# List products in the masks' slots, and a regrouped routing tail, in a masked-attention and expert kernel

## The chip, the cores and the metric

The kernel runs on one core of a Trainium2 chip. A core has five engines that run side by side, each through its own list of instructions in order: TensorE (PE, with PEld for its weight loads) multiplies matrices, VectorE (DVE) works elementwise, ScalarE (ACT) copies and applies functions, GpSimd (POOL) fills constants and issues the indirect DMAs, and SyncE (SP) issues DMAs. [...] ACT issues DMAs too, in its own order. The metric is the device time of one execution in microseconds (us); a comparison is made of several executions of each kernel.

## The reference, cut to what matters

The input `x` is 4096 rows of 512; `adj` is a 4096 x 4096 matrix of zeros and ones with few ones, denser in its first rows.

```python
adj = max(adj, eye)
q, k, v = layernorm(x) @ Wqs, Wks, Wvs          # 8 heads of 64
scores = q k^T / 8 + 0.01 * eye - 1e16 * (1 - adj)
x = x + sum_h softmax(scores) v Wo              # attention
xf = layernorm(x)
logits = xf @ Wg + bg                           # 8 experts
topk_scores, topk_idx = top_k(logits, 2)
w = softmax(topk_scores)
h = gelu(xf W1[e] + b1[e]);  y = h W2[e] + b2[e]
x = x + w[0] * y[topk_idx[0]] + w[1] * y[topk_idx[1]]
```

Only scores where `adj` is one count, and of the eight experts only two per row. The kernel computes just these.

## The kernel before, in words

Rows are handled in 32 tiles of 128. The work has three stages.

**Stage one** normalises `x`, projects it to keys, values and queries and writes them to DRAM (`kv_d`, `q_d`), and at the same time reads `adj` and makes of it, for every tile of queries, a list of the keys that it needs. It is paced by the f32 projections on PE. A slot is one program-level product of 128x512 (two passes in the trace); there are 384. Before each product `step()` runs the jobs that are registered for its slot (`job(slot, f)`), in the order in which they were registered, so the source writes every engine's order by hand. For chunk `h` of `adj` (four tiles of rows by 512 columns, 64 chunks) slot 5 + 5h holds `masks` (L478: four 16-bit products with 32-column weights), three slots later `turn_masks`. After eight chunks a group `g` of four tiles is complete; its jobs hang on slot `s` = 5 + 5h + 5: classes, counts, ranks (`places`, at s to s+8), then the lists (`group_lists`): `rows` and `values` on DVE, 16 one-hot tiles on DVE (`hot`, L281, five buffers), 16 sets of 16-bit products with 32-column weights on PE (`quads`, L294), a copy on ACT (`copy`, L303), and a transpose and key steps (`keys`, L308 to L315). A group follows another every 40 slots.

```python
job(s + 9, call, hold, "l", 0)              # rows
job(s + 10, call, hold, "l", 1)             # values
for x2 in range(NT // 2):
    job(s + 11 + 2 * x2, call, hold, "l", 2, x2)       # hot
    job(s + 16 + x2 // 2 * 4, call, hold, "l", 3, x2)  # quads
job(s + 44, call, hold, "l", 4)             # copy
job(s + 47, call, hold, "l", 5)             # keys
```

**Attention** takes two list steps at a time (a duo). GpSimd gathers the listed keys and values into a ring of 24 places in SBUF (L696); the ring lies where stage one's buffers were. PE turns the keys (L723), multiplies queries by keys (L760), ACT applies the exponential (L767), DVE the mask (L773), PE multiplies by values (L788). The main loop puts `scores` of the next duo, `turn` of the one three ahead and `values` of the present one, then the jobs registered with `at(n, i, job)` for this step. PSUM has three banks for all of this, taken in turn (`bank`).

When a tile of queries is done, `end_of` scales it (L810 to L812), turns it, projects it with `wo` (L828), adds `x` (L837), writes the row out and takes the statistics. When a group of tiles is done (seven of four tiles, then tiles 28 and 29, 30, and 31), `route` makes the second layernorm (`root`, `norm`, in place in the tile of `x`), the logits (`flip`, `gate`), the rank of each expert in a row (`rank`), its place in the expert's list (`place`, `number_places`, `keep_places`), the first and second choice (`pick(0)`, `pick(1)`: six DVE steps each; `weigh`: the difference of the two logits on DVE and its exponential on ACT, L1010 and L1011), the weights (`finish`), and the scatter of every row to the lists of its two experts in DRAM (`scatter`, L1029, on GpSimd, two per tile). A row carries four further words: its number, the place of its first choice, and the two weights. After the last group `totals` counts the rows for each expert and pads each list's end with a tile of blank rows: three on GpSimd, three on SP, two on ACT (L970, L985). The loop's steps past the last duo have no attention work.

Then the table of expert tiles is made on DVE with one product on PE (L1146 to L1182), a flag is computed (L1186 to L1198), and the **expert stage** begins: SP fetches the first four tiles (`fetch`, L1226), PE runs 60 transposes that serve nothing else (`warm`, L1296), DVE goes on with the table for half tiles (`halves`), and then for each of 66 tiles PE turns the rows (L1301), multiplies (L1341), turns (L1352), multiplies (L1370), and GpSimd adds the result into the output (L1392).

## Time and profile before

| what | us |
|---|---|
| median of three runs (2056.35 to 2059.91) | 2056.84 |
| the profiled execution | 2068.36 |
| its span in the trace | 2066.5 |
| PE busy | 1942.0 (94%) |
| DVE busy | 959.3 (46%) |
| ACT busy | 785.1 (38%) |
| GpSimd busy | 571.1 (28%) |
| stage one's last f32 product | about 465 |
| last step of attention's value products | about 1487 |
| first product of the expert stage | 1531.4 |

How to read it. The page's second part cuts the span into 40 slices; a digit is an engine's busy share in tenths, and the row of the clock gives the share of PE's full speed that was granted. In a timeline a row has the start, the length, engine, line, operation, output and inputs, shapes, the number of equal instructions merged, and in brackets the idle time of the engine before it with what ended it. PE's instructions are pipelined and their ends modelled, so one reads the difference of two starts. An engine that is mostly idle can still set the time where others wait for it.

### The profile page before, as it was taken

Reading aid. Unit: us, or ns where it says so; the run is one execution under the profiler, and the core shown is the slowest. Engines: PE = TensorE matmul, PEld = TensorE weight load, DVE = VectorE, ACT = ScalarE, POOL = GpSimd, SP = SyncE. Lnnn points to the kernel's source line nnn. Section 1 sums busy time; section 2 is a strip of 40 time slices with the busy share of each in tenths; the row PEclk is TensorE's granted clock in tenths of the full one; section 3 lists DMA queues with packets and bytes.
Section 4 is the critical chain, followed back from the end, with each engine's and each line's share of the span. In section 5 each row is a group of like instructions: output and inputs, shape, how many; then the busy total and the mean of one; then the engine's idle time right before and its main releaser. Section 6 shows DMA issues by size and latency. Waiting matters only on the chain. (4 is left out here: it accounts for less than half of the span.)

```text
span 2066.5 us, 59701 instructions
## 1 busy us (share of the span) xinstructions
PE 1942.0 (94%) x25491; PEld 1283.8 (62%) x25491; DVE 959.3 (46%) x2501; ACT 785.1 (38%) x1152; POOL 571.1 (28%) x721
## 2 busy tenths in 40 slices
PE   9899999998999998999999998998869999999996
PEld 4344444447888787887878787787644444444443
DVE  3455555534544464564545555464653333333332
ACT  3233233315555554644545454445312222222221
POOL 2000000015333426354272625333121222222221
PEclk9999999999999999999999999999979999999998
DMA  9877877339678849779596777868873555555532
GB/s 371 267 254 255 255 254 243 99 132 406 215 259 286 287 165 366 274 267 318 202 340 234 282 280 259 293 214 305 273 269 77 132 127 111 116 114 118 113 68 42
DMA packets 193410, 462.00 MB, mean 224 GB/s; under 512 B 30384, under 2 KB 46768, under 8 KB 193008
## 3 DMA queue, kind: packets, MB, share of 16 engines
q0 software_dynamic: 67024, 249.44, 37.6%
q1 hardware_dynamic: 101808, 177.51, 26.1%
q10 hardware_dynamic: 24304, 31.11, 4.3%
q8 instruction: 206, 3.38, 0.6%
q14 instruction: 68, 0.56, 0.1%
HBM read 385.37 MB, written 72.64 MB: 222 GB/s over the span
## 5 line engine op out<-in xcount | busy, mean ns | idle before, releaser
L696 POOL DMA_INDIRECT ring<-kv_d,idx x361 | 360.9, 1000 | 873.7 <-ACT l L303 437.1
L767 ACT ACTIVATE pr<-ps 128x1024 f32<-128x1024 f32 x270 | 270.4, 1025 | 376.1 <-PE ps L760 373.9
L773 DVE SCALAR_TENSOR_TENSOR pr<-t,pr 128x1024 f32<-128x1024 uint16 x238 | 284.5, 1223 | 243.8 <-ACT pr L767 243.7
L760 PE MATMUL ps<-q,kT 64*64 64x64 f32 (+1 forms) x10224 | 308.5, 237 | 26.4 <-issue 24.4
L788 PE MATMUL o<-ring,pr 128*64 128x65 f32 x8640 | 297.3, 226 | 26.9 <-issue 24.0
L760 PEld LDWEIGHTS ps<-q,kT 64*64 64x64 f32 (+1 forms) x10224 | 274.8, 149 | 69.5 <-issue 56.4
L788 PEld LDWEIGHTS o<-ring,pr 128*64 128x64 f32 x8640 | 273.9, 140 | 54.6 <-issue 49.4
L1341 PE MATMUL ph<-ring,xT 128*128 (+1 forms) x528 | 238.1, 594 | 0.8 <-ACT xT L1303 0.8
L723 PE MATMUL pkT<-ident,ring 128*128 128x128 f32 x1572 | 206.0, 280 | 12.7 <-DMA ring<-kv_d 6.0
L725 ACT COPY kT<-pkT 128x512 f32<-128x512 f32 (+1 forms) x270 | 198.5, 787 | 15.0 <-DMA q_d<-qT 6.7
L1392 POOL DMA_INDIRECT out_dram<-y,r x66 | 101.8, 1543 | 367.8 <-ACT y L1387 293.3
L723 PEld LDWEIGHTS pkT<-ident,ring 128*128 128x128 f32 x1572 | 171.0, 142 | 29.8 <-issue 7.7
L1370 PE MATMUL py_e<-ring,hT 128*128 (+1 forms) x396 | 182.3, 596 | 1.6 <-ACT hT L1363 1.6
L1341 PEld LDWEIGHTS ph<-ring,xT 128*128 128x128 f32 (+1 forms) x528 | 91.3, 183 | 99.9 <-issue 98.7
L1387 ACT ACTIVATE y<-y,wt 128x512 f32<-128x512 f32 x66 | 47.6, 722 | 269.5 <-DVE y L1383 229.7
L604 PE MATMUL pv<-wv,xT 128*128 128x512 f32 x256 | 131.3, 608 | 0.0
L604 PE MATMUL pk<-wk,xT 128*128 128x512 f32 x256 | 128.8, 614 | 0.7 <-ACT xT L399 0.7
L589 PE MATMUL pq<-xT,wq 128*128 128x512 f32 x256 | 125.9, 607 | 0.0
L1346 DVE COPY h<-ph 128x512 f32<-128x512 f32 x66 | 45.6, 692 | 169.9 <-PE ph L1341 169.9
L1029 POOL DMA_INDIRECT xs_d<-x,slot_i x64 | 70.2, 1097 | 186.6 <-DVE x L1025 159.3
L828 PE MATMUL py<-wo,oT 128*128 128x512 f32 x256 | 118.9, 607 | 1.4 <-ACT oT L822 0.7
L1370 PEld LDWEIGHTS py_e<-ring,hT 128*128 128x128 f32 (+1 forms) x396 | 67.2, 183 | 75.9 <-issue 74.1
(293 smaller groups left out, 1893.3 us busy)
## 6 DMA issues: line engine op xcount, KB each, us to landing
adj<-in_adj_dram SPq DMA_DIRECT2D x64, 1024.0 KB, 5.6
wo<-in_L_ffn_W_dram SPq DMA_DIRECT2D x72, 256.0 KB, 4.6
kv_d<-kvr ACTq DMA_DIRECT2D x32, 516.0 KB, 5.7
ring<-kv_d SPq DMA_DIRECT2D x32, 516.0 KB, 6.9
r<-xs_d SPq DMA_DIRECT2D x57, 258.0 KB, 2.6
ring<-in_L_ffn_W_dram SPq DMA_DIRECT2D x56, 256.0 KB, 5.2
xt<-in_x_dram SPq DMA_DIRECT2D x32, 256.0 KB, 6.3
q_d<-qT ACTq DMA_DIRECT2D x32, 256.0 KB, 2.8
```

The source lines that it names most:

```text
L589: nc.tensor.matmul(pq, w["q"][:, c, ts(p, P)], xTs[b][:, c, :], start=(c == 0), stop=(c == DC - 1),)
L604: nc.tensor.matmul(pk, xTs[b][:, c, ts(t, P)], w[n][:, c, :], start=(c == 0), stop=(c == DC - 1),)
L696: nc.gpsimd.indirect_dma_start(out=g, out_offset=None, in_=kv_d, in_offset=bass.IndirectOffsetOnAxis(ap=idx[i // GL][:, i % GL, a : a + 1] ...
L723: nc.tensor.transpose(pk[:, x * NP + p, :], g[:, ts(p, P)], ident)
L725: nc.scalar.copy(kT[:, : nk * NP], pk[:, : nk * NP])
L760: nc.tensor.matmul(ps[c : c + nk, r, p * P + x * nq : p * P + (x + 1) * nq], kT[r * KD : (r + 1) * KD, p, c : c + nk], q[r * KD : (r + 1) ...
L767: nc.scalar.activation(pr.rearrange("p h q -> p (h q)"), ps.rearrange("p r f -> p (r f)"), AF.Exp)
L773: nc.vector.scalar_tensor_tensor(pr, st["t"].unsqueeze(1).to_broadcast([P, H, P]), 0.0, pr, op0=ALU.is_gt, op1=ALU.mult,)
L788: nc.tensor.matmul(o[c * HALF : (c + 1) * HALF, h // NP, (h % NP) * VW : (h % NP + 1) * VW], pr[:, hd * NP + p, c * HALF : (c + 1) * HALF] ...
L828: nc.tensor.matmul(hold["py"], hold["oT"][:, c, :], wo[:, c, :], start=(c == 0), stop=(c == NP - 1),)
L1341: nc.tensor.matmul(ph[a], xTs[b][:, c, a], w, start=(c == 0), stop=(c == DC - 1), skip_group_check=b >= FULL,)
L1370: nc.tensor.matmul(py[a], hTs[b][:, c, a], w, start=(c == 0), stop=(c == HC - 1), skip_group_check=b >= FULL,)
```

## The change

It has these parts.

- Stage one: `rows` and `values` come one slot later; the products of two one-hot tiles stand at s+15, s+20, ..., s+50, five slots apart, which are the slots of `masks` (they are registered first, so they come directly ahead of them); the one-hots stand at 0 and 2 in each five slots; copy and keys come at s+52 and s+55.
- Routing: `pick` handles both choices in one set of steps of twice the width, with the exponential asked for after the fourth. A row now carries the place of its first choice, 1/(1+e) and e, where e is that exponential; the expert stage makes the weight from these with three steps instead of two. For the last two groups, of one tile each, these words are written straight into the row. The last three tiles' norms go to tiles of their own instead of in place.
- The order behind attention: the choices of tile 30 come one step later, so behind the rank of tile 31; jobs of the last duo's step run before its value products; 24, 8 and 30 transposes of the identity (`idle`) are put on PE after the last projection, after the last rank and after the totals.
- The blank rows: five on SP, and three on ACT behind the last choices; none on GpSimd.
- The table: two constants are made at the kernel's start, and a subtraction and a product become one step.

```diff
@@ -147,6 +147,13 @@
     nth = const.tile([P, 1], F32, name="nth")
     nc.gpsimd.iota(nth, pattern=[[0, 1]], base=0, channel_multiplier=1,
                    allow_small_or_imprecise_dtypes=True)
+    nth128 = const.tile([P, 1], F32, name="nth128")
+    nc.vector.tensor_scalar_mul(nth128, nth, float(P))
+    second01 = const.tile([P, 2], F32, name="second01")
+    nc.vector.memset(second01, 0.0)
+    nc.vector.memset(second01[:, 1:], 1.0)
+    none = const.tile([P, E], F32, name="none")
+    nc.vector.memset(none, 0.0)
@@ -555,13 +562,14 @@
                 job(s, ready)
                 for d, n in ((0, 0), (1, 1), (2, 2), (5, 3), (8, 4)):
                     job(s + d, call, hold, "p", n)
-                job(s + 9, call, hold, "l", 0)
-                job(s + 10, call, hold, "l", 1)
+                job(s + 10, call, hold, "l", 0)
+                job(s + 11, call, hold, "l", 1)
                 for x2 in range(NT // 2):
-                    job(s + 11 + 2 * x2, call, hold, "l", 2, x2)
-                    job(s + 16 + x2 // 2 * 4, call, hold, "l", 3, x2)
-                job(s + 44, call, hold, "l", 4)
-                job(s + 47, call, hold, "l", 5)
+                    m = 5 * (x2 // 2)
+                    job(s + 10 + m + 2 * (x2 % 2), call, hold, "l", 2, x2)
+                    job(s + 15 + m, call, hold, "l", 3, x2)
+                job(s + 52, call, hold, "l", 4)
+                job(s + 55, call, hold, "l", 5)
 
         def extras():
             nc.scalar.dma_start(out=wg, in_=Wg.rearrange("(c p) e -> p c e", p=P))
@@ -793,6 +801,11 @@
                         skip_group_check=True,
                     )
 
+        def idle(name, n):
+            t = bank(name, [NP, P])
+            for k in range(n):
+                nc.tensor.transpose(t[:, k % NP, :], ident, ident)
+
         groups = [list(range(g, g + 4)) for g in range(0, NT - 4, 4)] + [
             [NT - 4, NT - 3], [NT - 2], [NT - 1]
         ]
@@ -848,6 +861,8 @@
             at(n + 1, i, flip_o)
             at(n + 2, i, project)
             at(n + 2, i, residual)
+            if i == NT - 1:
+                at(n + 2, i, lambda: idle("idle_0", 24))
             g = group_of[i]
             if i == groups[g][-1]:
                 route(g, n + 3)
@@ -886,9 +901,12 @@
                 hold["l"] = small.tile([P, 4, E], F32, tag="l", name=f"l_{g}")
 
             def norm(k):
-                xi = xs_[m[k]]
+                xi = old = xs_[m[k]]
+                if m[k] >= NT - 3:
+                    xi = mid.tile([P, W], F32, tag="x", bufs=10, name=f"xn_{m[k]}")
+                    xs_[m[k]] = xi
                 nc.scalar.activation(
-                    xi[:, :D], xi[:, :D], AF.Identity, bias=hold["shift"][:, k : k + 1],
+                    xi[:, :D], old[:, :D], AF.Identity, bias=hold["shift"][:, k : k + 1],
                     scale=hold["y"][:, k : k + 1],
                 )
                 nc.gpsimd.iota(xi[:, D : D + 1].bitcast(I32), pattern=[[0, 1]],
@@ -964,65 +982,65 @@
-                for e in range(E):
-                    if e < 3:
-                        nc.gpsimd.memset(tick, 0.0)
-                        s = nc.gpsimd.indirect_dma_start(
-                            out=xs_d,
-                            out_offset=bass.IndirectOffsetOnAxis(ap=ends[:, e : e + 1], axis=0),
-                            in_=blank, in_offset=None,
-                        )
-                    else:
-                        eng, queue = (
-                            (mybir.EngineType.SP, nc.sync) if e < 6
-                            else (mybir.EngineType.Activation, nc.scalar)
-                        )
-                        last = nc.values_load(
-                            ends[0:1, e : e + 1], engines=(eng,), min_val=e * R,
-                            max_val=e * R + N,
-                            skip_runtime_bounds_check_because="counts of at most N",
-                        )
-                        s = queue.dma_start(out=xs_d[bass.ds(last, P), :], in_=blank)
+                closing["ends"] = ends
+                blanks(range(5), mybir.EngineType.SP, nc.sync)
+
+            def blanks(experts, eng, queue):
+                for e in experts:
+                    last = nc.values_load(
+                        closing["ends"][0:1, e : e + 1], engines=(eng,), min_val=e * R,
+                        max_val=e * R + N,
+                        skip_runtime_bounds_check_because="counts of at most N",
+                    )
+                    s = queue.dma_start(out=xs_d[bass.ds(last, P), :], in_=blank)
...
-            def pick(j):
-                r, l, pl = hold["rank"][:, :G], hold["l"][:, :G], hold["place"][:, :G]
-                if j == 0:
-                    hold["top"], hold["sl"] = small_tile("top", [2, 4]), small_tile("slot", [2, 4])
-                    hold["slot"] = small.tile(
-                        [P, 2, 4], I32, tag="slot_i", bufs=3, name=f"slot_i_{g}"
-                    )
-                top, slot = hold["top"], hold["sl"]
-                is_j = small_tile(f"is{j}", [4, E])
-                nc.vector.tensor_single_scalar(is_j[:, :G], r, float(j), op=ALU.is_equal)
-                got = small_tile(f"got{j}", [4, E])
-                nc.vector.tensor_mul(got[:, :G], is_j[:, :G], l)
-                nc.vector.tensor_reduce(top[:, j, :G], got[:, :G], axis=AX.X, op=ALU.add)
-                nc.vector.tensor_mul(is_j[:, :G], is_j[:, :G], pl)
-                nc.vector.tensor_reduce(slot[:, j, :G], is_j[:, :G], axis=AX.X, op=ALU.add)
-                nc.vector.tensor_copy(hold["slot"][:, j, :G], slot[:, j, :G])
-
-            def weigh():
-                top = hold["top"]
-                less = small_tile("less", [4])
-                nc.vector.tensor_sub(less[:, :G], top[:, 1, :G], top[:, 0, :G])
-                nc.scalar.activation(less[:, :G], less[:, :G], AF.Exp)
-                hold["less"] = less
+            def pick():
+                F = [P, 2, G, E]
+
+                def twice(a):
+                    return a.unsqueeze(1).to_broadcast(F)
+
+                is_ = small.tile([P, 2, 4, E], F32, tag="is", bufs=3, name=f"is_{g}")[:, :, :G]
+                nc.vector.tensor_tensor(
+                    is_, twice(hold["rank"][:, :G]),
+                    second01.unsqueeze(2).unsqueeze(3).to_broadcast(F), op=ALU.is_equal,
+                )
+                got = small.tile([P, 2, 4, E], F32, tag="got", bufs=3, name=f"got_{g}")[:, :, :G]
+                nc.vector.tensor_mul(got, is_, twice(hold["l"][:, :G]))
+                top = small_tile("top", [2, 4])
+                nc.vector.tensor_reduce(top[:, :, :G], got, axis=AX.X, op=ALU.add)
+                hold["less"] = xs_[m[0]][:, D + 3 : D + 4] if G == 1 else small_tile(
+                    "less", [4])[:, :G]
+                diff = small_tile("diff", [4])
+                nc.vector.tensor_sub(diff[:, :G], top[:, 1, :G], top[:, 0, :G])
+                nc.scalar.activation(hold["less"], diff[:, :G], AF.Exp)
+                nc.vector.tensor_mul(is_, is_, twice(hold["place"][:, :G]))
+                slot = small_tile("slot", [2, 4])
+                nc.vector.tensor_reduce(slot[:, :, :G], is_, axis=AX.X, op=ALU.add)
+                hold["slot"] = small.tile([P, 2, 4], I32, tag="slot_i", bufs=3, name=f"slot_i_{g}")
+                nc.vector.tensor_copy(hold["slot"][:, :, :G], slot[:, :, :G])
+                hold["sl"] = slot
+                if G == 1:
+                    nc.vector.tensor_copy(xs_[m[0]][:, D + 1 : D + 2], slot[:, 0, :1])
 
             def finish():
+
                 less, slot = hold["less"], hold["sl"]
                 more = small_tile("more", [4])
-                nc.vector.tensor_scalar_add(more[:, :G], less[:, :G], 1.0)
-                w2_ = small_tile("w2_", [2, 4])
-                nc.vector.reciprocal(w2_[:, 0, :G], more[:, :G])
-                nc.vector.tensor_mul(w2_[:, 1, :G], less[:, :G], w2_[:, 0, :G])
-                nc.vector.tensor_sub(w2_[:, 0, :G], w2_[:, 0, :G], w2_[:, 1, :G])
+                nc.vector.tensor_scalar_add(more[:, :G], less, 1.0)
+                if G == 1:
+                    nc.vector.reciprocal(xs_[m[0]][:, D + 2 : D + 3], more[:, :G])
+                    return
+                inv = small_tile("inv", [4])
+                nc.vector.reciprocal(inv[:, :G], more[:, :G])
                 for k in range(G):
                     xi = xs_[m[k]]
                     nc.vector.tensor_copy(xi[:, D + 1 : D + 2], slot[:, 0, k : k + 1])
-                    nc.vector.tensor_copy(xi[:, D + 2 : D + 4], w2_[:, :, k])
+                    nc.vector.tensor_copy(xi[:, D + 2 : D + 3], inv[:, k : k + 1])
+                    nc.vector.tensor_copy(xi[:, D + 3 : D + 4], less[:, k : k + 1])
 
             def scatter(k, j):
                 nc.gpsimd.memset(tick, 0.0)
@@ -1049,10 +1067,15 @@
             at(n + 1, m[-1], number_places)
             at(n + 1, m[-1], keep_places)
             if g == len(groups) - 1:
+                at(n, m[-1], lambda: idle("idle_1", 8))
                 at(n + 1, m[-1], totals)
-            at(n + 2, m[-1], lambda: pick(0))
-            at(n + 2, m[-1], lambda: pick(1))
-            at(n + 2, m[-1], weigh)
+                at(n + 1, m[-1], lambda: idle("idle_2", 30))
+            if g == len(groups) - 2:
+                n += 1
+            at(n + 2, m[-1], pick)
+            if g == len(groups) - 1:
+                at(n + 2, m[-1], lambda: blanks(
+                    range(5, E), mybir.EngineType.Activation, nc.scalar))
             at(n + 3, m[-1], finish)
             n += 4
             for k in range(G):
@@ -1117,6 +1140,9 @@
         while n < S or any(k >= n for k in later):
             duo(scores, n + 1)
             duo(turn, n + 3)
+            if n == S - 1:
+                for _, job in later.pop(n, []):
+                    job()
             duo(values, n)
             if n < S:
                 end = steps[duos[n][-1]]
@@ -1146,8 +1172,6 @@
         nc.vector.tensor_single_scalar(whole, number, 7, op=ALU.logical_shift_right)
         tiles_e = tail.tile([P, E], F32, name="tiles_e")
         nc.vector.tensor_copy(tiles_e, whole)
-        none = tail.tile([P, E], F32, name="none")
-        nc.vector.memset(none, 0.0)
         upto = tail.tile([P, E], F32, name="upto_e")
         nc.vector.tensor_tensor_scan(
             upto, tiles_e, none, initial=0.0, op0=ALU.add, op1=ALU.add
@@ -1158,8 +1182,9 @@
         nc.vector.tensor_reduce(ej[:, 0:1], past, axis=AX.X, op=ALU.add)
         nc.vector.tensor_mul(past, past, tiles_e)
         nc.vector.tensor_reduce(ej[:, 1:2], past, axis=AX.X, op=ALU.add)
-        nc.vector.tensor_sub(ej[:, 1:2], nth, ej[:, 1:2])
-        nc.vector.tensor_scalar_mul(ej[:, 1:2], ej[:, 1:2], float(P))
+        nc.vector.scalar_tensor_tensor(
+            ej[:, 1:2], ej[:, 1:2], -float(P), nth128, op0=ALU.mult, op1=ALU.add
+        )
         diag = tail.tile([P, 2, P], BF16, name="diag")
         nc.vector.tensor_mul(
             diag, ident.unsqueeze(1).to_broadcast([P, 2, P]),
@@ -1373,11 +1398,16 @@
                     )
             r = rows[b]
             wt = work.tile([P, 1], F32, tag="wt", name=f"wt_{b}")
+            rest = work.tile([P, 1], F32, tag="rest", name=f"rest_{b}")
             nc.vector.tensor_scalar(
-                wt, r[:, D + 1 : D + 2], pos[:, b : b + 1], r[:, D + 2 : D + 3],
-                op0=ALU.is_equal, op1=ALU.mult,
-            )
-            nc.vector.tensor_add(wt, wt, r[:, D + 3 : D + 4])
+                rest, r[:, D + 3 : D + 4], -1.0, 1.0, op0=ALU.mult, op1=ALU.add
+            )
+            nc.vector.tensor_scalar(
+                wt, r[:, D + 1 : D + 2], pos[:, b : b + 1], rest, op0=ALU.is_equal, op1=ALU.mult,
+            )
+            nc.vector.tensor_scalar(
+                wt, wt, r[:, D + 3 : D + 4], r[:, D + 2 : D + 3], op0=ALU.add, op1=ALU.mult
+            )
```

## The prediction

> **What bounds the kernel now.** I read the page's busy shares and slices first, then the busy time by stage, then the timeline where a stage begins or ends, and last the waits. TensorE (PE) is busy 94%; in stage one (to about 465 us) and in the expert stage (from 1530) it hardly pauses, and the hole is behind attention:
>
> ```profile
> PE 1942.0 (94%) x25491; PEld 1283.8 (62%) x25491; DVE 959.3 (46%) x2501; ACT 785.1 (38%) x1152; POOL 571.1 (28%) x721
> PE   9899999998999998999999998998869999999996
> ...
> PEclk9999999999999999999999999999979999999998
> ```
>
> So in stage one I price PE's own work. The timeline of PE there shows the list products (L294) and the mask products (L478) apart, and once side by side:
>
> ```profile
> 155.40 1.02 PE L604 MATMUL pk<-wk,xT 128*128 128x512 f32 x2
> 156.35 0.42 PE L294 MATMUL list<-oh,r_all 128*32 128x128 f16 x16
> 156.70 1.13 PE L604 MATMUL pk<-wk,xT 128*128 128x512 f32 x2
> 157.66 0.60 PE L492 MATMUL pwt<-ident,ws 128*128 128x128 f32 x4
> ...
> 163.05 1.02 PE L604 MATMUL pv<-wv,xT 128*128 128x512 f32 x2
> 163.91 0.60 PE L492 MATMUL pwt<-ident,ws 128*128 128x128 f32 x4
> ...
> 166.16 0.42 PE L294 MATMUL list<-oh,r_all 128*32 128x128 f16 x16
> 166.40 0.41 PE L478 MATMUL pwd<-adj,pw 128*32 128x512 bf16 x4
> ```
>
> Read starts, since ends are modelled. Two f32 passes between f32 neighbours take 0.86 (163.05 to 163.91), 0.95 before a list run and 0.96 behind one. A list run takes 0.35 alone and 0.24 with mask products behind it. So a separate run costs 0.09 + 0.35 + 0.10 = 0.54, a joined one 0.24: 0.30 us apiece.
>
> Behind attention nothing is busy; a chain of short DVE, ACT and PE steps sets the time, and its end is the 60 warm-up transposes (L1296):
>
> ```profile
> 1490.21 3.70 PE L828 MATMUL py<-wo,oT 128*128 128x512 f32 x8 [0.73 <-ACT oT L822]
> ...
> 1505.66 1.88 PE L910 MATMUL pl<-wg,x2T 128*128 128x8 f32 x8 [0.70 <-ACT x2T L903]
> ...
> 1521.52 8.61 PE L1296 MATMUL pt_warm<-ident 128*128 128x128 f32 x60 [0.24 <-DVE flag L1198]
> 1529.96 0.20 PE L1275 MATMUL pq_e<-diag,ones 128*128 128x22 bf16 x2
> 1530.01 0.64 PE L1301 MATMUL pt_e<-ident,r 128*128 128x128 f32 x4
> ```
>
> The first expert rows are fetched by SP at 1524.47 (waiting for GpSimd's last scatter, issued 1520.36 to 1521.32, to land) and land 3.0 later, at 1527.5: PE is 2.5 us behind them.
>
> [...] both 128*32 runs side by side save 0.30. [...] PE's clock reads 0.80 in 1495 to 1500, 0.50 to 1525 and 0.97 in 1525 to 1530, 3.8 us into the warm-up, where transposes go from 0.21 to 0.11 each. [...] here steps of 8 and of 64 elements both follow each other at about 0.2, so a step twice as wide is nearly free.
>
> **Part 1, stage one.** On PE the runs of 128*32 and other 16-bit products fall from 123 to 83: 40 fewer. 40 x 0.30 = **-12.0**. The products and copies are the same in number.
> Against it: a group's first list product now stands at slot +15 of its group instead of +16, in front of the masks. That is one f32 product (0.86), the masks (0.54) and the keys' transpose (0.22) earlier: 1.6. It needs DVE's second one-hot. DVE's work from the ranks to there is unchanged within 0.1: two one-hots of the group before come in (2 x 0.65) and the five key steps go out (1.24). Today PE arrives after the one-hot by 1.7, 2.0, 1.7, 0.5, 2.7, 2.1, 3.2 and 0.2 us in groups 0 to 7. So groups 0 to 6 lose 1.1 in all, in group 3; group 7, where PE has no masks to do and one more separate run, loses 0.5. **+1.6**. Behind DVE there queue the norm and the next rows' statistics, which have more slack. The rows step now waits for the last list product of the group before, in the same slot; DVE gets there at about the same time, so nothing.
>
> **Start of attention.** GpSimd's first gather waits for the last list copy:
>
> ```profile
> 451.60 0.27 ACT L303 COPY l<-list 128x128 f32<-128x128 f32 x1 [0.63 <-PE list L294]
> 452.46 1.07 POOL L696 DMA_INDIRECT ring<-kv_d,idx  x1 [437.05 <-ACT l L303]
> ...
> 465.47 1.94 PE L723 MATMUL pkT<-ident,ring 128*128 128x128 f32 x16 [0.73 <-issue]
> ...
> 472.06 2.48 ACT L725 COPY kT<-pkT 128x512 f32<-128x512 f32 x4 [6.70 <-DMA q_d<-qT]
> ```
>
> The copy moves from slot 369 to 377 of 384, so the first gather comes about 5.3 before the stage's end instead of 12.7: 7.4 later. What hides it is ACT's wait for the last query write, which holds the first copy until 6.9 after the end. By then 7 gathers have landed today; with DMA full (1.03 of its engines, 413 GB/s, 1.6 us for a gather) about 4 will have. PE takes them at the 4th first and needs the 7th at +12.3, the 10th at +16.0; they come at about +10 and +15 to +17. Bounds: -1 (the query write lands sooner with fewer gathers ahead of it) to +7.4 (cover gone). I take **+0.5**.
>
> **Part 2, choices in one set of steps.** Two picks of 6 steps and the difference (13) become 7, and the exponential waits for 4. At the group of tiles 24 to 27 PE stands 3.66 us (1471.6 to 1475.30), because its score bank waits for an ACT copy behind that exponential (1473.19); at 1374.8 it stands 0.7. Earlier groups show no PE stall. About 9 steps at 0.15 to 0.17: 1.35 at the former, counted in part 3; **-0.5** at the latter. Finishing has two steps more for four tiles, hidden behind PE.
>
> **Part 3, behind attention**, in the before trace's clock:
> - The projection of tile 30 ends 1.35 sooner, but its gate products (1.95) now precede the last value products, and root(30) (13 steps, 2.4) precedes the scaling of tile 31 on DVE. Projection of 31 starts at 1490.9, not 1490.2: 0.7 lost.
> - 24 idle transposes (24 x 0.11 = 2.6) hold the transpose of tile 30 until 1497.0. Today ACT copies it only at 1498.02, after issuing the output rows at 1497.57: hidden; root(31), behind the place number, ends 1500.3 instead of 1499.6.
> - The exponential, and behind it ACT's norm of 31, waits for 4 steps instead of 13: 1501.4, not 1502.95. Own tiles also drop its wait for the output write.
> - Logits of 31: transpose, copy, gate, at full clock 1504.6, at half 1505.9, today 1507.6.
> - The rank of 31 passes ahead of the choices of 30: counts final at 1506.5 to 1507.8, today 1511.4. Then two choices and finishes: table begins 1510.5 to 1511.7, today 1515.7.
> - The table has a memset and a step less (0.3): warm-up starts 1516.0 to 1517.2, today 1521.5.
> - Warm-up: 6.5 all at full clock, 8.2 to 9.8 if PE's pause since the idle transposes halved it again. Ready at 1522.5, or 1525.4 to 1527, today 1530.0.
> - Scatters: three blank rows leave GpSimd (3 x 1.27); its last scatter ends 1514.7, lands +3.1, fetch +3.0: 1520.8, hidden by the warm-up. SP's five blanks (0.9 each) and ACT's three land by 1517.
> I weigh full clock at a third: **-4.8** (bounds -1 and -7.5).
>
> **Part 4.** One more 0.16 us step in each of 66 expert tiles lies before DVE's wait for PE (158.6 us of such waits): 0; uncovered it is 10 us. Four set-up steps at the start lie in DVE's 0.43 wait for the first rows: 0.
>
> Sum: -12.0 + 1.6 + 0.5 - 0.5 - 4.8 = -15.2. On the profiled execution, 2068.4 (span 2066.5), that is 2053.2; it stands 11.5 above the median of 2056.8, so the forecast is 2056.8 - 15.2 = **2041.6**.
>
> **Rivals.**
> - *The cover is too thin (0.21).* DVE is late by 1.2 in each of eight groups (9.6 instead of 1.6) or the gathers' 7.4 reach PE: either leaves -7.2 to -8.3, 2049; both at once 2056. For: slacks of 0.5 and 0.2, DMA at its limit. Against: the query write covers 6.9.
> - *The clock holds behind attention (0.17).* Tail -7.5, total -18: 2039. For: 30 idle transposes before the table; against: 6 us with little PE work after them.
> - *Slower (0.04): PE's clock halves in stage one.* [...] It decides from 2.4 us a group (19.3 in all). [...] Against: the slacks above.
> - *The joined runs save nothing (0.08)*, because products of f16 and bf16 side by side differ from the 13 seen: then -3, 2054. Against: all 13 show 0.24 to 0.25.
>
> **Numbers.** The main case has 0.50: 2041.6, own range 2037 to 2046. 8 in 10 reaches to the rivals at 2039 and 2049: 2035 to 2050. 0.2% is 4.1 us, about what a measurement of this kernel can tell: slower by more only in the halved clock and mishaps like it, 0.05; within it, joined runs that save nothing or both covers gone, 0.08; faster 0.87.
>
> **What would show it.** Stage one's end about 10 earlier; list runs at 0.24 with mask products behind; stalls before L301 in groups 3 and 7 alone; first gather 5 before the stage's end and PE's first scores about 8 after it; from the start of tile 31's projection to the warm-up 25 to 26 us (today 31.3); expert stage unchanged per tile. Wrong if stage one ends less than 6 earlier, or if PE waits for the fetched rows instead of the warm-up.

## The result and the profile after

Over 20 executions each the median is 2050.25 us after and 2058.49 before; the ratio is 0.9952 (95% interval 0.994 to 0.9964), that is -9.9 us (-12.4 to -7.4). The forecast was -15.2. On the forecast's base of 2056.8 the ratio gives 2047.0, one past the main case's 2037 to 2046 and inside its wide range of 2035 to 2050.

The profiled execution after took 2048.19 (span 2046.3), 20.2 less than the one before (2068.36). That is twice the measured difference, so the two traces must be compared stage by stage. The page after, busy shares and slices:

```profile
PE 1936.2 (95%) x25553; PEld 1287.6 (63%) x25553; DVE 968.7 (47%) x2517; ACT 785.0 (38%) x1152; POOL 568.2 (28%) x715
...
PE   9799999998999998999999999998889999999996
...
PEclk9899999999999999999999999999989999999998
```

| stretch, from PE's starts (us) | before | after | difference |
|---|---|---|---|
| to stage one's last f32 product | 464.1 | 454.7 | -9.4 |
| from there to attention's first scores | 9.6 | 10.4 | +0.8 |
| first to last scores | 1002.6 | 996.0 | -6.6 |
| last scores to the first expert transposes | 53.7 | 49.4 | -4.3 |
| from there to the end | 536.5 | 535.9 | -0.6 |

The -6.6 inside attention can't be put down to the change. The traces record PE's clock as full or half. Up to the last expert tiles the half stretches (windows below) last 3.41 us (seven times before, six after), 6.83 (three and two), 10.24 (one and two) and 27.31 (once, before, behind attention). Between first and last scores it was at half for 36.6 us before and for 23.7 after, and half of that taken off (a warm-up transpose took 0.21 at half clock and 0.11 at full) leaves 984.3 and 984.2. This working is an estimate and rough: in the ten traces of the first two chips and of these two kernels (24 to 40 us at half clock) it leaves 978 to 987, so it doesn't show attention unchanged to within a few us. Over 68 executions of the kernel before, the correlation of time and mean granted clock is -0.59: the windows go with about a third of the scatter of the times.

**Stage one.** PE's timeline after: the list run (L301) stands directly ahead of the mask run (L485).

```profile
234.68 1.02 PE L597 MATMUL pq<-xT,wq 128*128 128x512 f32 x2
235.63 0.42 PE L301 MATMUL list<-oh,r_all 128*32 128x128 f16 x16
235.88 0.40 PE L485 MATMUL pwd<-adj,pw 128*32 128x512 bf16 x4
236.20 2.84 PE L597 MATMUL pq<-xT,wq 128*128 128x512 f32 x6
```

Starts: 0.95 before the list run, 0.25 for it, 0.32 for the masks. The trace has 53 such pairs, 13 before. The cost of a separate run belongs to its shape of 128*32, not to its 16 bits, for the trace has 16-bit products of 128*128 too:

```profile
163.79 1.13 PE L597 MATMUL pq<-xT,wq 128*128 128x512 f32 x2
164.75 0.33 PE L187 MATMUL tot<-cls,ones 128*128 128x384 bf16 x1
164.91 0.33 PE L190 MATMUL pre<-cls,below 128*128 128x384 bf16 x1
165.08 1.88 PE L597 MATMUL pq<-xT,wq 128*128 128x512 f32 x4
```

Single starts in the trace: an f32 pass ahead of `tot` or behind `pre` takes 0.43, as between f32 passes. The pass ahead of a list run takes 0.52, and the first one behind a list or mask run 0.53 (here the one at 163.79, behind masks).

**Start of attention.** The timeline after:

```profile
446.83 0.42 PE L301 MATMUL list<-oh,r_all 128*32 128x128 f16 x16
...
448.15 1.06 POOL L704 DMA_INDIRECT ring<-kv_d,idx  x1 [432.78 <-PE list L301]
...
449.34 0.27 ACT L310 COPY l<-list 128x128 f32<-128x128 f32 x1 [0.40 <-ACT qT L602]
...
459.20 0.66 PE L731 MATMUL pkT<-ident,ring 128*128 128x128 f32 x4 [2.12 <-DMA ring<-kv_d,idx]
...
463.36 2.48 ACT L733 COPY kT<-pkT 128x512 f32<-128x512 f32 x4 [7.44 <-DMA q_d<-qT]
```

The first gather follows the last list products and not their copy, which comes 1.2 behind it. It starts 6.5 before stage one's last product (454.7; before: 11.7). PE now waits for gathers (2.12), but ACT's first copy still waits for the query write until 463.4, so the first scores are only 0.8 late.

**Behind attention.** The timeline after, and SyncE's waits at the fetch (us in total, times, longest):

```profile
1475.85 3.70 PE L841 MATMUL py<-wo,oT 128*128 128x512 f32 x8 [0.73 <-ACT oT L835]
...
1488.90 1.88 PE L928 MATMUL pl<-wg,x2T 128*128 128x8 f32 x8 [0.70 <-ACT x2T L921]
...
1490.81 0.17 DVE L932 TENSOR_TENSOR l<-pl,bg_sb 128x8 f32<-128x8 f32 x1 [1.75 <-PE pl L928]
...
1502.13 8.44 PE L1321 MATMUL pt_warm<-ident 128*128 128x128 f32 x60 [0.24 <-DVE flag L1223]
...
1506.61 2.91 SPq L1251 DMA_DIRECT2D r<-xs_d  x4
...
1510.40 0.20 PE L1300 MATMUL pq_e<-diag,ones 128*128 128x22 bf16 x2
1510.46 0.64 PE L1326 MATMUL pt_e<-ident,r 128*128 128x128 f32 x4
```

```profile
SPq L1251 <- DMA xs_d<-blank: 3.3, 2, 2.3
...
SPq L1251 <- DMA xs_d<-xn,slot_i: 0.8, 1, 0.8
```

From tile 31's projection to the warm-up it is 26.3 (31.3 before). PE goes from the warm-up straight into the expert stage. But SP waits for the blank rows now: the fetch comes 6.3 after the last scatter has left GpSimd (1500.28), and was expected 3.1 after it.

### The profile page after: what moved, and what is told of

It is laid out like the page before. It is cut to its first block, busy times and chain, and to the rows that moved or that the text cites. A ratio compares the mean times of both kernels' runs of the same rounds, so it can differ in the third digit from the quotient of the medians.

```text
span 2046.3 us, 59873 instructions
## 1 busy us (share of the span) xinstructions
PE 1936.2 (95%) x25553; PEld 1287.6 (63%) x25553; DVE 968.7 (47%) x2517; ACT 785.0 (38%) x1152; POOL 568.2 (28%) x715
## 5 line engine op out<-in xcount | busy, mean ns | idle before, releaser
L781 DVE SCALAR_TENSOR_TENSOR pr<-t,pr 128x1024 f32<-128x1024 uint16 x238 | 284.1, 1223 | 238.1 <-ACT pr L775 238.1
L796 PE MATMUL o<-ring,pr 128*64 128x65 f32 x8640 | 295.2, 225 | 30.8 <-issue 30.8
L733 ACT COPY kT<-pkT 128x512 f32<-128x512 f32 (+1 forms) x270 | 198.5, 787 | 15.2 <-DMA q_d<-qT 7.4
L1422 POOL DMA_INDIRECT out_dram<-y,r x66 | 101.8, 1542 | 365.8 <-ACT y L1417 270.0
L1047 POOL DMA_INDIRECT xs_d<-x,slot_i x58 | 62.2, 1073 | 180.3 <-DVE x L1043 140.6
```

Source lines behind the costliest of these rows:

```text
L733: nc.scalar.copy(kT[:, : nk * NP], pk[:, : nk * NP])
L781: nc.vector.scalar_tensor_tensor(pr, st["t"].unsqueeze(1).to_broadcast([P, H, P]), 0.0, pr, op0=ALU.is_gt, op1=ALU.mult,)
L796: nc.tensor.matmul(o[c * HALF : (c + 1) * HALF, h // NP, (h % NP) * VW : (h % NP + 1) * VW], pr[:, hd * NP + p, c * HALF : (c + 1) * HALF] ...
```

## The experiments

Twelve kernels in three batches of four, each batch on another chip; the kernel before ran beside each batch. The times below are differences to it, from the ratios. The traces of the first two chips compare with those before and after; on the third chip attention took 1223 to 1245 us in every kernel (993 to 1005 on the others) and the kernel before 2303, with PE's clock at half for 215 to 243 us of attention. What that chip does differently is not known, so its stretches are compared only with each other.

**1. slots_only: the first part alone.** The kernel before, with this edit of the change:

```diff
-                    job(s + 16 + x2 // 2 * 4, call, hold, "l", 3, x2)
+                    job(s + 15 + 5 * (x2 // 2), call, hold, "l", 3, x2)
```

and the jobs around it as in the change.

> The kernel before with the list products' slots of the change alone. Theory A (the parts add up, attention itself is unchanged): stage one's last f32 product at 454.7 instead of 464.1, first scores 8.7 earlier, attention and tail as before; time -8.5 (-7 to -10). Rival B (attention gives part back, because the first gather starts 6.5 before stage one's end instead of 11.7): stage one -9.5 too, but the time only -4 to -6, and attention from its first to its last scores 3 to 5 longer.

Measured: -7.0 (-10.5 to -3.7); stage one ends at 452.6. From its last product to tile 0's projection it takes 102.8, against 99.3 before. The interval of the time holds theory A and rival B alike. B's longer beginning of attention is there, but attention as a whole is not longer in this trace (999.4 from the first to the last scores, 1002.6 before).

**2. tail_only: all but the first part.** The reverse edit in the changed kernel.

> The changed kernel with the list products in their old slots. Theory A: stage one ends at 464.1, from the last scores to the first expert transposes 49.4 instead of 53.7; time -4.5 (-3.5 to -5.5), and with the other part alone this makes up the whole change. Rival B: -4.5 as well, since nothing of it lies in attention. Rival C (the tail's gain is a matter of where the clock's windows fall, not of the steps): 51 to 54 for the tail, and a time within 2 of before.

Measured: -3.7 (-7.2 to -0.2); stage one ends at 464.1, 48.1 from the last scores to the expert stage. By this stretch rival C falls, which had 51 to 54; the time alone doesn't exclude it. But the old tail took 50.6 in slots_only and 53.7 in the trace before, so two traces of the same tail differ by about 3 us; whether the windows at half clock make that is not shown.

**3. slots_apart: same spacing, runs apart.**

```diff
-                    job(s + 15 + m, call, hold, "l", 3, x2)
+                    job(s + 16 + m, call, hold, "l", 3, x2)
```

with the other list jobs one slot later too.

> The changed kernel with every list job of stage one one slot later, so the same five-slot spacing, but a list run stands alone, one f32 product away from the masks. Theory A (a joined run saves 0.30): 40 runs come apart, and stage one ends 12 later, at 466.5 (no stall before a list product, which gives 1 back: 465.5 to 467); time +11 against the changed kernel, +1 to +2 against before. Rival D (what helps is the spacing and order, not the join): stage one ends at 455 to 458.

Measured: +4.7 (+1.6 to +8.0); stage one ends at 468.6, 14 later than after. Its timeline on PE:

```profile
241.86 0.41 PE L485 MATMUL pwd<-adj,pw 128*32 128x512 bf16 x4
242.20 1.12 PE L597 MATMUL pq<-xT,wq 128*128 128x512 f32 x2
243.25 0.41 PE L301 MATMUL list<-oh,r_all 128*32 128x128 f16 x16
243.60 1.98 PE L597 MATMUL pq<-xT,wq 128*128 128x512 f32 x4
```

The list run alone takes 0.35 again. The expectation overlooked that the edit parts all 53 pairs, the 13 of before too: 468.6 less 454.1 (the mean end of the eight kernels with the change's slots) is 14.5, and 14.5 / 53 = 0.27; PE's stalls before list products are 0.5 here and 2.3 after, and without that difference it is 0.31, against the 0.30 forecast. Stage one has 13.7 us at half clock here and 10.2 after, which can make 1.7 of the 14. The join is what saves; rival D falls.

**4. no_idle: without the idle transposes.**

```diff
-                at(n + 2, i, lambda: idle("idle_0", 24))
-                at(n, m[-1], lambda: idle("idle_1", 8))
-                at(n + 1, m[-1], lambda: idle("idle_2", 30))
```

> The changed kernel without its 62 idle transposes. Theory A' (read from the trace after: the gate product of tile 31 takes 1.88 at half clock and the warm-up 8.3 with its first 3.4 at half clock in spite of them): the tail from the last scores to the first expert transposes stays at 49.4 within 0.5, and the time is the changed kernel's within 1. Rival E (they keep the clock up for the table's products and the start of the warm-up): warm-up of 9.5 or more, tail +1.5 to +3.

Measured: -8.9 (-12.4 to -5.2), and 48.9 instead of 49.4 from the last scores. As A' expected, and with a reason it did not have: the norm of tile 31 starts 0.95 and the warm-up 1.2 earlier, since neither the transpose of tile 30 is held nor the small product behind it, on which DVE's root of tile 31 waits (1.41 in the trace after); the warm-up then takes 0.7 longer, with 4.9 us at half clock instead of 3.4.

**5. last_group_early: early gathers again.**

```diff
+                if h == NHC - 1:
+                    job(s + 9, call, hold, "l", 0)
+                    ...
+                        job(s + 16 + x2 // 2 * 4, call, hold, "l", 3, x2)
```

In this kernel the last group's `rows` are written before the last products of the group before read the same buffer, so the lists of tiles 24 to 27 are partly made of wrong rows; the amount of work is the same.

> The changed kernel with the last group's lists in their old slots (no masks are left there to join), so the first gather comes 11 to 12 before stage one's last f32 product again instead of 6.5. Theory G (the later gathers cost attention's first steps about 2.5 beyond the start of the scores: from stage one's last product to the projection of the second tile, less half of the time at half clock, the four kernels with late gathers show 149.1 to 150.2, the two with early ones 147.1 and 147.4): 147.3 within 0.7, and a time 2 to 4 under the changed kernel's. Rival H (the cover by the query write was enough, the rest is chance): 149 to 150, and a time within 1 of it.

Measured: -7.4 (-10.7 to -3.9), no better than the changed kernel. Stage one ends at 459.7: DVE makes the last group's rows ahead of one-hots of the group before, and PE stands 3.1 until 410.4. The clock-corrected measure of the expectation gives 146.6, but kernels 6 and 7, with late gathers, give 146.6 and 146.5: it is no measure, since PE's half-clock time there falls in waits in part (in the trace after 2.6 of the 6.8 us from 461.4). Uncorrected, to tile 0's projection, it is 98.8, with 99.3 and 99.0 in the two others with early gathers and 99.9 to 102.8 in the seven with late ones. The clock doesn't make this difference: with 6.8 us at half clock in the stretch it is 99.3 and 99.0 with early gathers, 101.1 and 101.8 with late ones; with 10.2 it is 98.8 with early, 99.9 to 101.8 with late ones.

**6. two_picks: the choices in two sets of steps.**

```diff
+                for j in range(2):
+                    nc.vector.tensor_single_scalar(is_j[:, :G], r, float(j), op=ALU.is_equal)
+                    ...
```

> The changed kernel with the two choices in two sets of steps again (13 steps ahead of the exponential instead of 4, 5 or 6 more in all). Theory of the sum: the stall before the last scores grows from 3.2 to about 4.6; from the start of tile 31's projection to the first expert transposes +1.8 (two more sets on the path, 0.9 each), so 35.4 to 37 instead of 34.6 from the first projection product's start. Rival (DVE waits there anyway): within 0.5.

Measured (one execution): 39.4 from tile 31's projection to the expert transposes instead of 34.6, more than expected. Each of the two last sets takes 2.0 instead of 1.3, but the norm of tile 31 is 2.05 later before that, because ACT's exponential ahead of it waits for the whole set of tiles 28 and 29. The expectation had left that out (the prediction had it).

**7. blanks_back: blank rows on three queues.**

```diff
-                blanks(range(5), mybir.EngineType.SP, nc.sync)
+                for e in range(3):
+                    ...
+                    s = nc.gpsimd.indirect_dma_start(out=xs_d, ...)
+                blanks(range(3, 6), mybir.EngineType.SP, nc.sync)
+                blanks(range(6, E), mybir.EngineType.Activation, nc.scalar)
```

> The changed kernel with the blank rows as before: three on GpSimd ahead of the last scatters, three on SP, two on ACT ahead of the last choices. Theory V (the volume binds: eight blanks and the last scatters fill the DMA engines until 1505.3 whatever the queue, the fetch follows 1.2 later): fetch 5 to 6 after the last blank's or scatter's issue as now, first expert transposes 0 to +1. Rival S (GpSimd's serial issue binds): last scatter 3.8 later, first expert transposes +3 to +3.5, PE waits for the rows. Rival of the prediction (hidden by the warm-up): 0.

Measured (one execution): the last scatter leaves GpSimd 3.5 later, but the fetch comes only 0.8 later; expert transposes 1.9 later, of which 0.85 is in the steps ahead of the warm-up and 1.0 in the warm-up, with 5.6 us at half clock. Rival S falls, but neither of the others fits: V had 0 to +1, with the fetch 5 to 6 after the last issue, and the prediction's rival 0. The fetch comes 3.6 after the last scatter has left, and SP's wait ahead of it (4.9) is for the scatters here, not for the blank rows. So taking three blanks off GpSimd bought 0.8 at the fetch.

**8. half_blanks: half as many blank rows, a shorter warm-up.**

```diff
-                    s = queue.dma_start(out=xs_d[bass.ds(last, P), :], in_=blank)
+                    s = queue.dma_start(out=xs_d[bass.ds(last, Q), :], in_=blank[:Q])
-            for k in range(60):
+            for k in range(36):
```

> The changed kernel with blank rows of half a tile (the expert stage reads at most 63 of them behind a list, since the rest of a list goes in half tiles) and a warm-up of 36 transposes instead of 60. Theory V: 1.06 MB less is 2.8 less of DMA, so the fetch comes about 2.5 earlier, rows are there 5 after the flag, and the first expert transposes come 2 to 3 earlier against the flag (8.3 between warm-up start and expert stage becomes 5.5 to 6.5). Rival: the fetch waits for the last scatter and comes 0.5 earlier; then PE stands before the first expert transposes, and 7.5 to 8.3 stay between.

Measured (one execution): the warm-up ends 2.6 sooner, the fetch comes 0.2 sooner, and PE waits 1.7 for the rows; the gain is 0.8. V falls in its size: half the bytes, and the fetch comes hardly sooner. SP takes 6.1 for its five issues instead of 5.0, so the last blank leaves 1.1 later, and the fetch follows it by 4.9 instead of 6.2. The DMA engines are busy nearly as long: 0.90 of their time in the 8 us from 1505.4, moving 251 GB/s, where after it is 0.99 in the 8 us from 1497.0 at 362 GB/s. So half the bytes took more than half of their time; why is open.

**9 to 12, on the third chip.** last_group_fast puts the last group's products three slots apart, behind those of the group before:

```diff
+                if h == NHC - 1:
+                    ...
+                        job(s + 16 + 3 * (x2 // 2), call, hold, "l", 3, x2)
+                    job(s + 39, call, hold, "l", 4)
```

> The changed kernel with the last group's list products three slots apart instead of five (at +16 to +37, copy at +39, keys at +42, behind the last products of the group before). Theory G (late first gathers cost attention's beginning: from stage one's last product to the projection of tile 0 it takes 100.0 to 102.8 in the seven kernels with late gathers, 99.3 and 98.9 in the two with early ones): first gather 12 or more before stage one's end, 98 to 99.5 to the projection of tile 0, time 2 to 4 under the changed kernel's. Rival H (chance, or other places of the ring come free no earlier): 100.5 or more, time within 1 of it.

early_choice and in_place each take out one piece:

```diff
-            if g == len(groups) - 2:
-                n += 1
```

> The changed kernel with the choices of tile 30 ahead of the rank of tile 31 again. Theory of the sum: eight DVE steps (1.35) go ahead of the rank, so the totals and the first blank rows come 1.35 later, the table 0.4 later (the steps themselves are the same in number); since fetched rows are ready hardly before the warm-up ends, the first expert transposes come 0.4 to 1.3 later: 35.0 to 36 from the projection of tile 31. Rival (the order among DVE's steps is free): 34.6 within 0.3.

```diff
-                if m[k] >= NT - 3:
-                    xi = mid.tile([P, W], F32, tag="x", bufs=10, name=f"xn_{m[k]}")
-                    xs_[m[k]] = xi
```

> The changed kernel with the last three norms in place again. Theory of the sum: the output row of tile 31 is issued at 1482.5 and its norm starts at 1486.2, so the write has landed by then and nothing changes: 34.6 within 0.4 from the projection of tile 31. Rival (the write takes 4 or more to complete, as the last scatters do): norm and logits of tile 31 0.5 to 1.5 later, 35.1 to 36.

best joins five edits:

```diff
-            at(n + 2, m[-1], pick)
+            at(n + (1 if g == len(groups) - 2 else 2), m[-1], pick)
-                    nc.scalar.dma_start(out=b1T[:, e], ...)
+                    nc.gpsimd.dma_start(out=b1T[:, e], ...)
-                blanks(range(5), mybir.EngineType.SP, nc.sync)
+                blanks(range(4), mybir.EngineType.SP, nc.sync)
```

with ACT's blanks 4 to 7, all twelve transfers of that slot on GpSimd, the last group as in last_group_fast, without `idle_0`, and 48 warm-up transposes.

> The changed kernel with five edits: the last group's lists three slots apart; the ten extra loads in slot 40 (small weights, biases, blank rows) issued by GpSimd instead of ACT; the choices of tile 30 ahead of the logits of tile 31, in DVE's 1.75 of waiting; no idle transposes behind the last projection; four blank rows each on SP and ACT, and 48 warm-up transposes. Expected: the stall of 10.5 before the totals' product near 70 goes, and with it two or three windows at half clock (-12 to -14 by stage one's end: 440 to 442); attention's start -2; tail -2: a time 14 to 18 under the changed kernel's, 2033 to 2037. Rival (behind the extra loads the next thing is as late, a load of the mask or the same queue): stage one -3 to -5, time -7.

Measured: last_group_fast -3.5 (-7.8 to +0.7), best -14.7 (-20.5 to -9.2), the other two in one execution each, 2296.5 and 2308.7. Both times miss what was expected: 2 to 4 and 14 to 18 under the changed kernel's would be about -12 to -14 and -24 to -28 against the kernel before, and the intervals hold neither. The marks behind attention, from the start of tile 31's projection (the table's is its first step on DVE):

| kernel | norm of 31 | table | warm-up | its length | fetch | expert transposes |
|---|---|---|---|---|---|---|
| before | 12.7 | 25.5 | 31.3 | 8.3 | 34.3 | 39.8 |
| after | 10.35 | 20.5 | 26.3 | 8.2 | 30.8 | 34.6 |
| tail_only | 11.3 | 21.4 | 26.85 | 6.5 | 31.6 | 34.8 |
| no_idle | 9.4 | 19.5 | 25.1 | 8.8 | 29.7 | 34.1 |
| two_picks | 12.4 | 24.3 | 29.8 | 9.4 | 33.2 | 39.4 |
| last_group_fast (this tail as after) | 12.8 | 23.0 | 31.0 | 8.7 | 33.5 | 39.9 |
| early_choice | 11.95 | 21.4 | 29.8 | 8.5 | 31.5 | 38.5 |
| in_place | 12.35 | 22.3 | 30.5 | 8.5 | 32.4 | 39.25 |
| best | 10.9 | 20.0 | 28.6 | 6.5 | 30.3 | 35.3 |

The last four rows are the third chip's. Neither early_choice nor in_place is later than last_group_fast, which has the changed kernel's tail: the order of the choices and the own tiles gain nothing that can be seen in one trace each. early_choice's expectation of totals 1.35 later is wrong: from the logits of tile 31 to the lists' ends it takes 3.43, and 3.46 in last_group_fast, because in the changed order too DVE makes tile 30's choices before it reads the totals. The order that gains is the one in best: there these choices stand ahead of the logits of tile 31, in time in which DVE waits, and the lists' ends come 2.50 behind these logits.

In the two kernels of this chip with early gathers it takes 112.3 and 113.3 to tile 0's projection, in the two with late ones 116.0 and 117.3. This repeats what the other chips show, while last_group_fast's whole time does not show it.

best's stages do at least what was expected of them, though its time doesn't. Stage one's stall, after and in best (PE's row on the line of `tot`, ACT's ahead of it):

```profile
61.14 6.90 ACTq L579 DMA_DIRECT2D b1T<-in_L_ffn_b_dram  x6
...
69.13 0.27 ACT L503 CAST words<-pwt 128x128 uint16<-128x128 f32 x1 [13.56 <-DMA b1T<-in_L_ffn_b_dram]
...
70.99 0.48 PE L187 MATMUL tot<-cls,ones 128*128 128x384 bf16 x1 [10.37 <-DVE cls L182]
```

```profile
60.48 0.33 PE L187 MATMUL tot<-cls,ones 128*128 128x384 bf16 x1
```

The twelve small transfers (the expectation says ten) held ACT for 13.6, and with it PE. On GpSimd, which issues them from 16.7 to 26.0 and so some 40 us earlier, they hold nobody. Stage one ends at 441.0, against 454.4, 454.7 and 456.8 in the three others of this chip, and the tail is 4.6 shorter than last_group_fast's. Beside last_group_fast that makes 20 by the traces, where the times differ by 11 (-14.7 less -3.5, with intervals of 4 to 6 on either side); whether attention on that chip gives the rest back is not settled. The changed kernel itself was not timed on that chip, so that best beats it is not shown; it rests on best's -14.7 against the kernel before and on the stages.

## Why the prediction was right in kind and too large

It held that the parts add up, and they do. From the traces alone, each kernel against the kernel before (99.1 and 52.2 are the means of the two kernels with the old slots, and of the two with the old tail):

| kernel | stage one's end, -464.1 | to tile 0's projection, -99.1 | last scores to expert stage, -52.2 | sum | timed (interval) |
|---|---|---|---|---|---|
| after | -9.4 | +1.9 | -2.8 | -10.3 | -9.9 (-12.4 to -7.4) |
| slots_only | -11.5 | +3.7 | (old) | -7.8 | -7.0 (-10.5 to -3.7) |
| tail_only | 0 | (old) | -4.1 | -4.1 | -3.7 (-7.2 to -0.2) |
| slots_apart | +4.5 | +2.7 | -4.0 | +3.2 | +4.7 (+1.6 to +8.0) |
| no_idle | -11.0 | +2.7 | -3.3 | -11.6 | -8.9 (-12.4 to -5.2) |
| last_group_early | -4.5 | -0.3 | -2.7 | -7.5 | -7.4 (-10.7 to -3.9) |

All six sums lie in the measured intervals. Each stretch is from one trace, and the two old tails behind the 52.2 differ by 3, so the agreement to within 1 of most rows is in part luck. Term by term the means give -10.0, +2.4 and -3.4, -11.0 in all, where the prediction had -10.4, +0.5, -0.5 and -4.8. By the prediction's terms:

- *Joined runs, -12.0, and one-hot stalls, +1.6: right in sum, the stalls by luck.* Stage one ends at 452.6 to 454.7 in the eight kernels with these slots, 454.1 in the mean: -10.0 against -10.4. The stalls are near the size forecast (2.3 in the trace after) but not in its place: none is at a group's first product in groups 3 and 7. They are at the last product of groups 1, 2, 4 and 6, where DVE is already in the next group's ranks:

```profile
222.90 0.30 PE L301 MATMUL list<-oh,r_all 128*32 128x128 f16 x8
...
223.45 0.69 DVE L288 TENSOR_TENSOR oh<-sp,count 128x1024 f16<-128x1024 f16 x1
...
224.19 0.30 PE L301 MATMUL list<-oh,r_all 128*32 128x128 f16 x8 [0.99 <-DVE oh L288]
```

  The working looked at DVE ahead of the first product and took the later ones as free; the wider spacing had moved the last one into the next group.
- *Start of attention, +0.5: the mis-sized term, 2.4 in the mean of the seven kernels with late gathers on the first two chips (+0.8 to +3.7).* The cover by the query write was sized right for the first scores (0 to +0.8). What failed is the step that stops there: the gathers stay late behind the first scores (the 17th comes 5.9 to 7.8 behind them, 1.1 before; the 41st 53.0 to 55.1, 51.5 before), so PE pays on to tile 0's projection. The lateness itself was read too large. The prediction has the first gather wait for the list copy, eight slots later and 7.4 us; it waits for the last products, which moved from slot 369 to 375, and its lead on stage one's end fell by 5.1, from 11.7 to 6.5. A smaller lateness thus cost more than was forecast, and still less than the bound of +7.4.
- *Pick at 1374, -0.5: not seen;* it is below the scatter of attention.
- *Behind attention, -4.8 (a third and two thirds of the two cases give -5.0): right in its parts, less in sum.* Table at 20.5 (19.6 to 20.8 forecast), warm-up at 26.3 (25.1 to 26.3), expert stage at 34.6 (half clock: 34.5 to 36.1). But in five kernels with the new tail it is 48.1 to 49.4 against 50.6 and 53.7, -3.4 in the means: from the last scores to tile 31's projection it takes 1.3 more (0.7 forecast), and the idle transposes, costed as hidden, hold the norm of tile 31 by 0.95. The full-clock case could not pay: in tail_only the warm-up ran at full clock in 6.5, and PE stood for the rows:

```profile
1509.29 6.77 PE L1320 MATMUL pt_warm<-ident 128*128 128x128 f32 x60 [0.24 <-DVE flag L1222]
...
1514.04 2.92 SPq L1250 DMA_DIRECT2D r<-xs_d  x4
...
1517.26 0.63 PE L1325 MATMUL pt_e<-ident,r 128*128 128x128 f32 x4 [1.16 <-DMA r<-xs_d]
```

  The step that failed there is "SP's five blanks and ACT's three land by 1517": from tile 31's projection that is 26, and the fetch that waits for them comes at 30.8. In the trace after, SP's last blank is issued by 1500.4 and the fetch goes out at 1506.6, 6.2 later. For most of this the transfers are still under way: packets of the blank rows and of the scatters move until 1505.3, with the DMA engines 0.99 busy from 1497.0 to 1505.0, and 1.3 are left between the last packet and the fetch. The forecast has no term for the engines' time.
- *What made the tail shorter* is mostly the one-set choices: undoing them gives 3.8 of the table's 5.0 back, in one execution. The order of the choices was to bring the counts to 1.9 behind the logits of tile 31 instead of 3.8. PE does have them after 2.25 instead of 3.87, but DVE reads them behind the choices of tile 30 in either order: 0.

Of the rivals, the thin cover came nearest in time (2049), by its second half, the gathers, and to a third of its size. The joined runs do save, and PE's clock was at half in stage one no longer than before (10.2 us in both traces).

## What to carry to other kernels

Put short products of one tile shape side by side: here that was 0.3 us for every 128*32 run joined, with the products the same in number. When a producer is moved later behind a cover, follow the lateness past the end of the cover, to where the buffers are full again. And before an order is costed, ask who reads the result and what stands ahead of that reader on its own engine.

## What the runs showed of the hardware

- A run of 128*32 products between products of 128*128 cost 0.09 us in front and 0.10 behind (traces before and after: an f32 pass takes 0.52 and 0.53 there, 0.43 between f32 passes). 16-bit products of 128*128 between f32 ones cost neither (0.43).
- Twelve small transfers issued by ACT, eight of them reading single words (packets of 4 bytes), held ACT 13.6 us in the trace after; the eight took 1.4 us each there and 0.75 on GpSimd in best. PE stood 10.4 us for it, with 10.2 us at half clock around it. With GpSimd issuing them, and earlier, stage one ended 13 to 16 us sooner than in three others on the same chip.
- 62 transposes that serve nothing else kept PE's clock up only in part: with them 10.2 us at half clock lay between tile 31's projection and the warm-up (6.8 to 11.5 in the other traces of the first two chips that have them), without them (no_idle) 15.6, and the warm-up was 0.7 shorter; they delayed it by 1.2.
- Eight writes of 258 KB, issued from two queues within 5.1 us, together with the last scatters, kept the DMA engines busy until 4.9 us after the last issue, and the next reader started 1.3 us later (trace after). With half the bytes (half_blanks) the engines moved 251 GB/s instead of 362, and the reader started 0.2 us sooner.
- On one of the three chips of the experiments the same attention took 1223 to 1245 us instead of 993 to 1005, with stretches of 24 us at half clock.
